# Roots as powers on GpSimd, and additional maxima spread over steps, in a four-layer fp32 kernel

## The chip, the core and the metric

The kernel runs on one core of a Trainium2 chip. The metric is the device time of one execution in microseconds. Engines are named as in the profile: PE (matrix products), DVE (vector), ACT (activation functions), POOL (GpSimd), SP (the queue that issues most transfers). PEclk is the TensorE clock that was granted, as a share of full speed.

## What is computed

Everything is fp32. The input is x of 8 batches x 512 tokens x 256 channels, and four residual layers follow one another:

```python
x = x + attn(_layernorm(x))          # ProbSparse: top 307 of 512 queries by max - mean of the scores
x = x + ffn(_layernorm(x))           # 16 blocks of 64 hidden units, the top 4 of each token
x = attn_b(x)                        # gated linear attention, then SwiGLU, each behind an RMS norm
x = x + ffn(_layernorm(x))           # the blocked FFN again
```

Square roots occur in five places: in each layernorm, `(x - m) / sqrt(v + eps)`; in the RMS norms, whose root is added to an epsilon before it divides; and in the gated linear attention, where each head's output of 16 elements is normalized:

```python
var = jnp.mean((o - mu) ** 2, axis=-1, keepdims=True)
o = (o - mu) / jnp.sqrt(var + LN_EPS)
```

In the first attention, the maximum over keys of each query's scores decides which queries are kept: the scores are computed twice, once for the maxima and once for the exponentials.

## The kernel before

**Attention** (0 to about 552 us). The work is laid out in 128 steps, one for each batch (8), half of the channels (m), every second head (e) and quarter of the queries or keys (k). A step issues four maxima, one for each of four heads (`max_one`: two matrix products at L582, then a DVE reduction at L588) for its own position, and the exponentials (`exp_one`: three products at L608, an ACT Exp at L615 into a tile of tag "e", ten buffers) of the position 16 steps earlier (LAG), and the weighing of the values (`weigh`, L630) of the position before that. Between them, piece by piece, stands `front(b)`, which prepares a later batch: the normalized x is transposed (L415), projected to queries and keys (L435), and each of these is split into a high and a low half (`halves`: ACT L446 and L452, POOL L453) in tiles of tag "half", four buffers, which transfers (SP) then move to their places. When the maxima of a group are complete, `place_maxima` turns them (POOL L548, PE L554) and writes the thresholds of the kept queries into the "top" tiles, also of tag "half" (ACT L558 and L562, POOL L570 and L571).

Which group is placed in which step is put on a list in `all_maxima`. Near the end, from step 112 on, in every fourth step four further maxima are issued in one burst behind the step's own, so that the last maxima are done some steps early. `add_bias(b)` adds the output bias to a batch's x on POOL (L398); for batches 0 to 2 it stands in step 11, for the others four steps before their front begins.

Batches 1 and later are normalized by `one_by_root`: a reciprocal root computed on POOL with an integer first guess and three Newton rounds, 14 small instructions (L278 to L286) in all. Batch 0 has a root of its own (L342), which the change leaves as it is.

**The rest** (from about 592 us). The tokens are cut in four slices k. The blocked FFN, then the gated linear attention `gla(k)`, SwiGLU and the FFN again run slice by slice; pieces of the routing of the next slices and of `gla` are put between PE's long runs of matrix products. The scheduler decides the order of the instructions on each engine at build time, and each engine works through its own in that order. PSUM buffers made by `bank_l` (two in all) serve the projections (`project`: PE L1226, ACT copy L1231, DVE gate addition L1232), the transposes of o (L1348) and others in turn.

In `gla`, `heads(m)` computes o for one half of the channels: the products and reductions of DVE, POOL and ACT, then the squares (ACT L1326), o times the gate (POOL L1327) and the sum of the squares by head (DVE L1328) into `var[:, m]`. When both halves are done, ACT takes the root of the whole of var (L1335), DVE its reciprocal (L1336), and DVE multiplies o by it (L1339), one half after the other. PE transposes o after that.

`stats` (L69, L70), which the FFNs and `gla` use, takes a root on ACT and its reciprocal on DVE; `gla` has two further roots on ACT, rr (L1171) and r2 (L1380). ACT holds the tables of one set of functions at a time; where the next function is of another set, a table load stands ahead of it.

Of the kernel before, what the change touches and what calls it, by code (L numbers as in the profile page):

```python
# [10 lines left out]
F32 = mybir.dt.float32  # L11
HALF = mybir.dt.float32r
U8 = mybir.dt.uint8
I32 = mybir.dt.int32
# [26 lines left out]
def block_kernel(ctx: ExitStack, tc: tile.TileContext, t: dict, out: bass.AP):  # L41
# [13 lines left out]
    root = keep.tile([P, 1], F32, name="root")  # L55

    nc.scalar.activation(root, eps, AF.Sqrt)
    ident = keep.tile([P, P], F32, name="ident")
    make_identity(nc, ident)

    def stats(pool, srcs, n, tag):

        st = pool.tile([P, n, 6], F32, tag=tag + "_st", name=tag + "_st")
        mv = pool.tile([P, n, 2], F32, tag=tag + "_mv", name=tag + "_mv")
        rs = pool.tile([P, n], F32, tag=tag + "_rs", name=tag + "_rs")
        for i, src in enumerate(srcs):
            nc.vector.bn_stats(st[:, i, :], src)
            nc.vector.bn_aggr(mv[:, i, :], st[:, i, :])
        nc.scalar.activation(rs, mv[:, :, 1], AF.Sqrt, bias=eps)  # L69
        nc.vector.reciprocal(rs, rs)  # L70
        return mv, rs

    def normalize(dst, src, mv, rs, i):
# [33 lines left out]
    with ExitStack() as outer:  # L107
# [75 lines left out]
        with ExitStack() as inner:  # L183
# [86 lines left out]

            def one_by_root(rs, var, scale):

                n = rs.shape[1]
                v = a1.tile([P, n], F32, tag="ln_v", name="ln_v")
                u = a1.tile([P, n], F32, tag="ln_u", name="ln_u")
                nc.gpsimd.tensor_scalar(v, var, scale, LN_EPS, ALU.mult, ALU.add)  # L278
                nc.gpsimd.tensor_scalar(
                    rs.bitcast(I32), v.bitcast(I32), -0.5, float(0x5F3759DF), ALU.mult, ALU.add  # L280
                )
                for _ in range(3):
                    nc.gpsimd.tensor_tensor(u, v, rs, ALU.mult)
                    nc.gpsimd.tensor_tensor(u, u, rs, ALU.mult)
                    nc.gpsimd.tensor_scalar(u, u, -0.5, 1.5, ALU.mult, ALU.add)
                    nc.gpsimd.tensor_tensor(rs, rs, u, ALU.mult)  # L286

            def sum_stats(b, late):

# [99 lines left out]
            def move(dst, src, eng):  # L389

                eng.dma_start(out=dst.bitcast(I32), in_=src.bitcast(I32))

            fronts = {}
            bo = a1.tile([P, D], F32, name="bo")

# [7 lines left out]
            def front(b, pick, alone):  # L403
# [35 lines left out]

                def halves(ps, bias, early):  # L440

                    hi, lo = (
                        a2.tile([P, L], F32, tag="half", name=f"half{b}", bufs=4)
                        for i in range(2)
                    )
                    nc.scalar.activation(hi.bitcast(HALF), ps, AF.Identity, bias=bias)  # L446
                    if early:
                        nc.vector.scalar_tensor_tensor(
                            lo.bitcast(HALF), ps, bias, hi, ALU.add, ALU.subtract
                        )  # L450
                    else:
                        nc.scalar.activation(lo, ps, AF.Identity, bias=bias)  # L452
                        nc.gpsimd.tensor_tensor(lo.bitcast(HALF), lo, hi, ALU.subtract)  # L453
                    return hi, lo
# [86 lines left out]
            def place_maxima(b, m, es, tiles=range(4)):  # L541


                pt = bank_m(f"mxT_ps{b}")
                ks = slice(tiles[0], tiles[-1] + 1)
                cols = slice(P * ks.start, P * ks.stop)
                for e in es:
                    nc.gpsimd.tensor_copy(  # L548
                        apart.rearrange("p k (j r) -> p k j r", r=32)[:, ks, :, 2 * e : 2 * e + 2],
                        mx[:, b % 2, m, e, :].rearrange("p (k j) -> p k j", j=4)[:, ks]  # L550
                        .unsqueeze(3).to_broadcast([P, len(tiles), 4, 2]),
                    )
                for k in tiles:
                    nc.tensor.transpose(pt[:, bass.ts(k, P)], apart[:, k, :], ident)  # L554
                whole, hi = (
                    a2.tile([P, L], F32, tag="half", name=f"top{b}", bufs=4) for i in range(2)
                )
                nc.scalar.mul(whole[:, cols], pt[:, cols], -1.0)  # L558
                for e in es:
                    r = row_of(b, m, e)  # L560
                    nc.sync.dma_start(out=neg[r : r + 4, cols], in_=whole[2 * e :: 32, cols])
                nc.scalar.mul(hi[:, cols].bitcast(HALF), pt[:, cols], -1.0)  # L562

                top = tops[(2 * b + m) % 3][:, cols].bitcast(HALF)
                if b == NB - 1:
                    nc.vector.scalar_tensor_tensor(
                        top, hi[:, cols], less_odd, whole[:, cols], ALU.mult, ALU.add
                    )
                else:
                    nc.gpsimd.tensor_scalar(hi[:, cols], hi[:, cols], less_odd, None, ALU.mult)  # L570
                    nc.gpsimd.tensor_tensor(top, hi[:, cols], whole[:, cols], ALU.add)  # L571
# [146 lines left out]
                    place_maxima(*full.pop(0)[1])  # L718

            coming = 0  # L720

            def all_maxima(step):

                nonlocal coming
                coming += 1
                b, m, e, k = step
                if coming > len(steps) - 2:
                    full.append((n + 1, (b, m, (e,), (range(3), range(3, 4))[k - 2])))
                elif k == 3 and b == NB - 1 and m == 1:
                    full.append((n + 2, (b, m, (e,))))  # L730
                elif k == 3 and e == 1:
                    full.append((n + 2, (b, m, (0, 1))))
                if coming == len(steps):
                    place_full(n + 2)
                    top_queries()

            for n in range(len(steps) + LAG + 1):
# [32 lines left out]
                if here is not None:  # L770
                    last_exps = es[3][0:1, 0:1]
                if ahead is not None:
                    all_maxima(ahead)
                    if n >= 112 and n % 4 == 0 and coming < len(steps):
                        ahead = steps[coming]
                        together([max_one(*ahead, i, bank_m) for i in range(4)])
                        all_maxima(ahead)

                if n < FIRST:
                    if n in loads:  # L780
                        load_after(loads[n], maximum_of(n))
                    if n in (2, 5):
                        clear_values(n // 2, maximum_of(n))
                    if n == 1:
                        for _ in early[1]:
                            pass
                    if n > 1:
                        next(early[2], None)
                    if n == 9:
                        nc.gpsimd.tensor_copy(bo[0:1, 0:1], maximum_of(n))  # L790
                        nc.sync.dma_start(out=bo, in_=t["L0_attn_a_bo"].partition_broadcast(P))
                    if n == 11:
                        for b in range(3):
                            add_bias(b)
                    if n == 12:
                        build_spread(maximum_of(n))
                    while done < 22 * (n + 1) // FIRST:
                        next(pieces, None)
                        done += 1
                else:  # L800
                    if n >= LAG:
                        next(later, None)
                    if i == 12 and 0 <= batch < NB - 3:
                        norm(batch + 3)
                        add_bias(batch + 3)
                    if i == 0 and 0 <= batch < NB - 2:
                        pieces = front(batch + 2, bank_m, False)
                    if not empty:
                        next(pieces, None)
# [352 lines left out]
    def heads_of(x, axis="n"):  # L1162
        return x.rearrange(f"p {axis} (h d) -> p ({axis} h) d", d=DH)

    def gla(k):
# [2 lines left out]
        yield  # L1168

        rr = small("rr")  # L1170
        nc.scalar.activation(rr, mv[:, :, 1], AF.Sqrt)  # L1171
        nc.vector.tensor_tensor(rr, rr, rs, ALU.mult)
        nc.vector.tensor_scalar(rr, rr, RMS_EPS, None, ALU.add)
        nc.vector.reciprocal(rr, rr)
# [94 lines left out]
        def heads(m):  # L1269
# [56 lines left out]
            nc.scalar.activation(sq, o[m], AF.Square)  # L1326
            nc.gpsimd.tensor_tensor(o[m], o[m], gate, ALU.mult)  # L1327
            nc.vector.tensor_reduce(var[:, m, :], heads_of(sq), AX.X, ALU.add)  # L1328
            yield


        var = rest.tile([P, NC2, NB * P // DH], F32, tag="var", name="var")
        for m in range(NC2):
            yield from heads(m)
        nc.scalar.activation(var, var, AF.Sqrt, bias=eps, scale=1.0 / DH)  # L1335
        nc.vector.reciprocal(var, var)  # L1336
        oT = rest.tile([P, 2, NC2, 512], F32, tag="made", name="oT")
        for m in range(NC2):
            nc.vector.tensor_tensor(  # L1339
# [37 lines left out]
        r2 = small("r2")  # L1377
        nc.vector.tensor_tensor(r2, mv[:, :, 0], mv[:, :, 0], ALU.mult)
        nc.vector.tensor_tensor(r2, r2, mv[:, :, 1], ALU.add)
        nc.scalar.activation(r2, r2, AF.Sqrt)  # L1380
        nc.vector.tensor_scalar(r2, r2, RMS_EPS, None, ALU.add)
        nc.vector.reciprocal(r2, r2)
        yield
# [111 lines left out]
```

## Time and profile before

| | us |
|---|---|
| three runs: median (lowest to highest) | 1603.43 (1598.21 to 1610.94) |
| the profiled execution, its time | 1599.7 |
| the profiled execution, its span | 1598.0 |
| mean granted clock of the profiled execution | 0.98 |
| a table load on ACT | 1.283 |
| reduction of var, 128x64 from 128x1024, DVE (L1328) | 1.22 |
| reciprocal of var, 128x128, DVE (L1336) | 0.95 |
| root of var, 128x128, ACT (L1335) | 0.40 |

In the lines of the profile, a group of instructions is named by its line, its engine and what it writes from what it reads. "<-" in square brackets names what ended the idle time ahead of an instruction. A line of the waits says which instruction waited for which other: microseconds in all, how many times, the longest. A line of the busy table gives for a stretch of time what each engine was busy, the number of its instructions in brackets, and then PEclk, the share of the transfer engines and GB/s.

### The profile page before, as it was taken

What the parts mean: (1) busy time and instruction counts of PE and PEld (TensorE: products, weight loads), DVE (VectorE), ACT (ScalarE), POOL (GpSimd) and SP (SyncE); (2) the same over time, 40 slices, a digit from 0 to 9 for tenths busy, and PEclk for the clock granted to TensorE, in tenths of its full rate; (3) what the DMA queues carried; (4) which work ended last, traced back from release to release, by engine and by line L of the source; (5) the groups of instructions that cost most, each with busy time, mean ns of one, the idle gap of its engine ahead of it and who ended that gap; (6) DMA issues with size and microseconds to landing.
All of it is one profiled execution on the core that took longest, in us unless ns stands there. A gap on an engine that the chain in (4) does not pass through costs nothing.

```text
span 1598.0 us, 21558 instructions
## 1 busy us (share of the span) xinstructions
PE 1547.5 (97%) x7982; PEld 860.5 (54%) x7982; DVE 943.9 (59%) x1974; ACT 704.5 (44%) x1290; POOL 454.5 (28%) x547
## 2 busy tenths in 40 slices
PE   6799999999999999999999999999999999999999
PEld 3344444444444376655564556546545655767666
DVE  6688776776776974547744566467275532354332
ACT  4377777677765843442255225432631542221110
POOL 4653453452220241123433233234243210000000
PEclk9899999999996999999999999999999999999999
DMA  5301112112110051100000001000000010011100
GB/s 188 122 16 68 42 42 81 42 42 81 42 42 2 3 171 27 40 2 13 1 0 0 0 2 27 0 0 1 1 1 1 0 28 1 23 31 40 40 27 27
DMA packets 38553, 52.65 MB, mean 33 GB/s; under 512 B 9068, under 2 KB 22580, under 8 KB 38448
## 3 DMA queue, kind: packets, MB, share of 16 engines
q1 hardware_dynamic: 37648, 50.09, 9.6%
q8 instruction: 63, 1.03, 0.3%
q10 hardware_dynamic: 800, 1.18, 0.2%
q14 instruction: 42, 0.34, 0.1%
HBM read 21.24 MB, written 4.33 MB: 16 GB/s over the span
## 4 chain that ended last, share of the span: by engine, by line
PE 78%; DVE 11%; ACT 4%; POOL 4%; issue 2%; DMA 2%; SPq 0%; ACTq 0%; POOLq 0%; DVEq 0%
PE y_ps L1087 17%; PE h_ps L1113 11%; PE s L608 10%; PE av L630 8%; PE swi_ps L1140 8%; PE proj_ps L1226 7%; PE s L582 5%; DVE pr L1259 2%; PE v_ps L505 2%; DVE pr L1249 2%; PE gla_y L1356 2%; PE q_ps L435 2%; PE k_ps L435 2%; POOL o L1276 1%; PE chT_ps L944 1%
## 5 line engine op out<-in xcount | busy, mean ns | idle before, releaser
L588 DVE TENSOR_REDUCE mx<-s 128x1 f32<-128x512 f32 x512 | 325.8, 684 | 119.2 <-PE s L582 118.1
L615 ACT ACTIVATE e<-s 128x512 f32<-128x512 f32 x512 | 276.0, 600 | 127.5 <-PE s L608 121.1
L1087 PE MATMUL y_ps<-w,h 128*128 128x256 f32 x1024 | 236.6, 387 | 8.2 <-DVE h L1122 7.6
L1113 PE MATMUL h_ps<-xnT,w 128*128 128x512 f32 x512 | 228.2, 594 | 0.0
L1087 PEld LDWEIGHTS y_ps<-w,h 128*128 128x128 f32 x1024 | 194.8, 193 | 48.8 <-DVE h L1122 13.2
L1113 PEld LDWEIGHTS h_ps<-xnT,w 128*128 128x128 f32 x512 | 94.7, 190 | 105.8 <-issue 103.8
L630 PE MATMUL av<-e,va 128*32 128x512 f32 (+1 forms) x1216 | 148.7, 559 | 2.1 <-ACT st L640 2.0
L582 PE MATMUL s<-km,qh 32*128 32x512 f32 x512 | 137.5, 508 | 8.5 <-DMA km<-half 4.4
L1121 ACT ACTIVATE h<-h_ps,b 128x512 f32<-128x512 f32 x96 | 65.3, 685 | 176.7 <-PE h_ps L1113 176.7
L1122 DVE TENSOR_TENSOR h<-h,mk 128x512 f32<-128x512 f32 x128 | 94.1, 749 | 82.7 <-ACT h L1121 62.0
L608 PE MATMUL s<-qh,km 32*128 32x512 f32 x512 | 139.4, 508 | 0.9 <-ACT e L615 0.8
L1098 DVE TENSOR_TENSOR xres<-xres,y_ps 128x512 f32<-128x512 f32 x47 | 32.2, 685 | 155.1 <-PE y_ps L1087 117.9
L1140 PE MATMUL swi_ps<-zT,w_up 128*128 128x512 f32 x256 | 122.4, 597 | 0.3 <-DVE h L1149 0.3
L1140 PE MATMUL swi_ps<-zT,w_gate 128*128 128x512 f32 x256 | 121.6, 593 | 0.0
L1087 PE MATMUL y_ps<-w_down,h 128*128 128x256 f32 x512 | 117.5, 380 | 0.0
L1226 PE MATMUL proj_ps<-q_w,rT 128*128 128x512 f32 x256 | 115.3, 594 | 0.5 <-ACT al L1209 0.4
L608 PE MATMUL s<-ql,km 32*128 32x512 f32 x512 | 112.9, 408 | 0.0
L608 PE MATMUL s<-tops,takes 4*128 4x512 f32 x512 | 110.3, 402 | 0.0
L582 PE MATMUL s<-km,ql 32*128 32x512 f32 x512 | 110.2, 412 | 0.0
L582 PEld LDWEIGHTS s<-km,qh 32*128 32x128 f32 x512 | 55.5, 187 | 101.5 <-DVE mx L588 68.4
L1087 PEld LDWEIGHTS y_ps<-w_down,h 128*128 128x128 f32 x512 | 95.1, 190 | 19.0 <-issue 7.4
L1146 ACT ACTIVATE h<-swi_ps 128x512 f32<-128x512 f32 x64 | 38.1, 595 | 139.9 <-PE swi_ps L1140 139.7
(235 smaller groups left out, 2186.9 us busy)
## 6 DMA issues: line engine op xcount, KB each, us to landing
mk<-md SPq DMA_DIRECT2D x32, 256.0 KB
qh<-half SPq DMA_DIRECT2D x63, 128.0 KB
ql<-half SPq DMA_DIRECT2D x63, 128.0 KB
km<-half SPq DMA_DIRECT2D x63, 128.0 KB
out<-xres SPq DMA_DIRECT2D x15, 256.0 KB
xres<-in_L_attn_a_x SPq DMA_DIRECT2D x7, 512.0 KB
w<-in_f_w1T SPq DMA_DIRECT2D x1, 1024.0 KB
w<-in_f_w2T SPq DMA_DIRECT2D x1, 1024.0 KB
```

The source lines that it names most:

```text
L435: nc.tensor.matmul(ps, w[:, c, bass.ts(m, P)], x[:, c, :], start=(c == 0), stop=(c == NC2 - 1),)
L582: nc.tensor.matmul(s, (qh, ql)[i].bitcast(HALF)[rows, e, bass.ts(k, P)], km.bitcast(HALF)[rows, e, :], start=(i == 0), stop=(i == 1),)
L588: nc.vector.tensor_reduce(mx[:, b % 2, m, e, r : r + 1], s, AX.X, ALU.max)
L608: nc.tensor.matmul(s, keys.bitcast(HALF), queries.bitcast(HALF), start=(i == 0), stop=(i == 2),)
L615: nc.scalar.activation(ex, s, AF.Exp, scale=1.0 / DH**0.5)
L630: nc.tensor.matmul(av[32 * j : 32 * j + 32, queries], va[:, 8 * kt + 4 * m + j, DH * e : DH * e + 2 * DH], es[j][:, queries], start=(kt == ...
L1087: nc.tensor.matmul(y[0][:, bass.ts(i, D)], h[f][:, bass.ts(2 * u + i, P)], w[:, f, :], start=(f == 0), stop=(f == NF - 1),)
L1113: nc.tensor.matmul(ps, w1[:, c, bass.ts(f, P)], xT[g][:, c, :], start=(c == 0), stop=(c == NC2 - 1),)
L1121: nc.scalar.activation(hf, ps, AF.Relu, bias=b1[:, f : f + 1])
L1122: nc.vector.tensor_tensor(hf, hf, mk[g][:, f, :], ALU.mult)
L1140: nc.tensor.matmul(ps, w[:, c, bass.ts(f, P)], zT[g][:, c, :], start=(c == 0), stop=(c == NC2 - 1),)
L1226: nc.tensor.matmul(ps, rT[b // G4][:, c, bass.ts(b % G4, P)], q_w[:, c, m], start=(c == 0), stop=(c == NC2 - 1),)
```

## The change

All roots but those of batch 0's normalization become powers on POOL: `to_power(x, p)` raises a tile to 0.5 or -0.5 in place, with the exponent as a tile that is broadcast. `one_by_root` shrinks to two instructions. The root of var is taken for each m on its own, right behind its reduction. The root activation of ACT and the reciprocal of DVE go in `stats` and for var; for rr and r2 the root goes, and the reciprocal stays.

In the attention, the halves tiles of batches 0 and 1 and the first pair of top tiles use the buffers of tag "e". The further maxima are issued one a step (two from step 120 on) instead of four in every fourth, with the placement of the last batch's first half one step later. The biases of batches 0 to 2 are added in steps 18, 22 and 26 instead of 11.

```diff
+    def to_power(x, p):
+
+        nc.gpsimd.tensor_tensor(x, x, p.to_broadcast(list(x.shape)), ALU.pow)
+
...
-        nc.scalar.activation(rs, mv[:, :, 1], AF.Sqrt, bias=eps)
-        nc.vector.reciprocal(rs, rs)
+        nc.gpsimd.tensor_scalar(rs, mv[:, :, 1], LN_EPS, None, ALU.add)
+        to_power(rs, less_half)
...
-                n = rs.shape[1]
-                v = a1.tile([P, n], F32, tag="ln_v", name="ln_v")
-                u = a1.tile([P, n], F32, tag="ln_u", name="ln_u")
-                nc.gpsimd.tensor_scalar(v, var, scale, LN_EPS, ALU.mult, ALU.add)
-                nc.gpsimd.tensor_scalar(
-                    rs.bitcast(I32), v.bitcast(I32), -0.5, float(0x5F3759DF), ALU.mult, ALU.add
-                )
-                for _ in range(3):
-                    nc.gpsimd.tensor_tensor(u, v, rs, ALU.mult)
-                    nc.gpsimd.tensor_tensor(u, u, rs, ALU.mult)
-                    nc.gpsimd.tensor_scalar(u, u, -0.5, 1.5, ALU.mult, ALU.add)
-                    nc.gpsimd.tensor_tensor(rs, rs, u, ALU.mult)
+                nc.gpsimd.tensor_scalar(rs, var, scale, LN_EPS, ALU.mult, ALU.add)
+                to_power(rs, less_half)
...
+            def half_tile(first, name):
+
+                tag, bufs = ("e", 10) if first else ("half", 4)
+                return a2.tile([P, L], F32, tag=tag, name=name, bufs=bufs)
...
-                    hi, lo = (
-                        a2.tile([P, L], F32, tag="half", name=f"half{b}", bufs=4)
-                        for i in range(2)
-                    )
+                    hi, lo = (half_tile(alone, f"half{b}") for i in range(2))
...
-                whole, hi = (
-                    a2.tile([P, L], F32, tag="half", name=f"top{b}", bufs=4) for i in range(2)
-                )
+                whole, hi = (half_tile(b + m == 0, f"top{b}") for i in range(2))
...
-                    full.append((n + 2, (b, m, (0, 1))))
+                    full.append((n + 2 + b // (NB - 1), (b, m, (0, 1))))
...
-                    all_maxima(ahead)
-                    if n >= 112 and n % 4 == 0 and coming < len(steps):
-                        ahead = steps[coming]
-                        together([max_one(*ahead, i, bank_m) for i in range(4)])
+                    if n >= 112 and n % 4 == 0 and coming + 1 < len(steps):
+                        extra = [(*steps[coming + 1], i) for i in range(4)]
                         all_maxima(ahead)
+                        all_maxima(steps[coming])
+                    else:
+                        all_maxima(ahead)
+
+                    for _ in range(2 if n >= 120 else 1):
+                        if extra:
+                            together([max_one(*extra.pop(0), bank_m)])
...
-                    if n == 11:
-                        for b in range(3):
-                            add_bias(b)
...
+                    if n in (18, 22, 26):
+                        add_bias((n - 18) // 4)
...
-        nc.scalar.activation(rr, mv[:, :, 1], AF.Sqrt)
+        nc.gpsimd.tensor_copy(rr, mv[:, :, 1])
+        to_power(rr, half_power)
...
             nc.vector.tensor_reduce(var[:, m, :], heads_of(sq), AX.X, ALU.add)
+            nc.gpsimd.tensor_scalar(
+                var[:, m, :], var[:, m, :], 1.0 / DH, LN_EPS, ALU.mult, ALU.add
+            )
+            to_power(var[:, m, :], less_half)
             yield
...
-        nc.scalar.activation(var, var, AF.Sqrt, bias=eps, scale=1.0 / DH)
-        nc.vector.reciprocal(var, var)
...
-        nc.scalar.activation(r2, r2, AF.Sqrt)
+        to_power(r2, half_power)
```

In the changed build, SP's order of transfers is the same as before; table loads on ACT number 20 instead of 45.

## The prediction

> **What bounds the kernel now.** I read the page first (shares, slices), then the busy table by stretch, then the waits of PE, then the timelines of DVE, POOL and ACT around each root.
>
> ```profile
> span 1598.0 us, 21558 instructions
> PE 1547.5 (97%) x7982; PEld 860.5 (54%) x7982; DVE 943.9 (59%) x1974; ACT 704.5 (44%) x1290; POOL 454.5 (28%) x547
> PE   6799999999999999999999999999999999999999
> PEclk9899999999996999999999999999999999999999
> ```
>
> PE is the bound: 97% busy, so only some 50 us of it stand idle, and beside them there is the time in which it is busy at a lower clock (slices 1 and 12). ACT, from which the change takes work, is 44% busy. A gain can come only from PE's idle time and from its clock. The stretches that hold both (columns: PE, PEld, DVE, ACT, POOL busy, granted clock):
>
> ```profile
> 50.00:55.00 5.00, 3.93 (x18) 1.34 (x16) 3.86 (x9) 1.19 (x2) 3.93 (x17) 1.00 0.76 260
> 55.00:60.00 5.00, 0.73 (x8) 0.28 (x6) 3.52 (x6) 1.19 (x3) 3.70 (x4) 0.92 0.60 165
> 60.00:65.00 5.00, 4.87 (x16) 3.03 (x17) 0.00 (x0) 1.89 (x5) 4.78 (x6) 0.50 0.42 158
> 480.00:482.00 2.00, 1.34 (x10) 0.48 (x9) 1.40 (x3) 0.42 (x1) 0.00 (x0) 1.00 0.01 4
> 486.00:511.00 25.00, 24.69 (x154) 10.19 (x150) 13.16 (x23) 12.60 (x25) 1.17 (x3) 0.50 0.01 2
> ```
>
> The waits of PE (us in all, times, longest), and from ACT's timeline the wait behind one of them:
>
> ```profile
> PE xnT_ps L415 <- DVE xn L319: 6.7, 1, 6.7
> PE v_ps L505 <- ACT half L452: 4.4, 1, 4.4
> PE oT_ps L1348 <- DVE o L1339: 4.4, 2, 2.5
> PE s L582 <- DVE mx L588: 2.5, 4, 0.8
> PE xnT_ps L415 <- POOL xn L319: 2.0, 4, 1.3
> 58.81 0.69 ACT L446 ACTIVATE half<-q_ps,bq 128x512 fp32r<-128x512 f32 x1 [5.77 <-POOL tops L571]
> ```
>
> The 6.7 us wait is the first load and stays. The other 13.3 us are what the change can reach.
>
> **The change part by part** (against the profiled execution: 1599.7 us, span 1598.0; the median of the three runs is 1603.4, 3.7 more, which I add at the end).
>
> *Table loads.* The order of the changed kernel has 20 loads in place of 45: 25 x 1.283 us (the row of L1335's loads) = 32 us of ACT. ACT is nowhere the engine that PE waits for in these stages (its waits above are on DVE and POOL), so I cost this at 0. The cover is ACT's 56% of free time. The Trainium skill ("ScalarE: Activation LUTs", What ACT_TABLE_LOAD costs) puts a switch at 2.66 us, load and drain; the timeline has the load at 799.44 and the root at 800.73, 1.29 later, with no drain to see. By the page 66 us of ACT would go, by the trace 32; at 0 on the path both give 0.
>
> *Start, one_by_root.* Fourteen POOL instructions (0.20 each, 0.28 apart, 3.8 us from 49.64 to 53.60; for batch 1 with a halves product between them, 29.95 to 35.01) become two. At 35.0 xn of batch 1 comes about 2 us earlier, which takes most of PE's 2.0 us wait on POOL xn. *Halves.* At 53.10 ACT is ready for batch 1's halves, but all four "half" buffers are held until POOL's tops L571 ends at 58.78: ACT waits 5.77, PE 4.41 (55.7 to 60.13), and the clock is then 0.50 until about 66 and near 0.57 from 72 to 80. In tag "e" (ten buffers, no exponential yet alive) this wait goes. Next late is DVE: four maxima take 2.48 us a step and DVE is otherwise full from 36 to 56, so a floor remains; the maxima of step 16, which end at 75.4 now, I put at 65. The biases (2.37 us each on POOL, three in a row from 61.95) hold up batch 1's second halves product (68.90) and its values (70.12), for which PE's weighing waits in turn. In the changed order of POOL the product stands ahead of them, the values between them (two biases, two value additions, the third bias, two more), so that cover is only partly gone: 2 x 2.37 still lie ahead of the first value. SP's order is unchanged; no transfer is moved past another. Start in all: -10, with -6 (DVE binds at once) and -13 (the second low-clock stretch goes too) as ends.
>
> *Additional maxima.* Now four come in one burst at n=112, 116, 120, so DVE has eight in a row (8 x 0.62 = 5.0 us in a 3.2 us step), and PE waits 2.5 us in all. One a step is 5 x 0.62 = 3.1, under the step; two at n=120 and 121 are 3.7, over it by 0.5 each. So -2.5 + 1 from waits. After the third burst the clock goes to 0.50 from 482.5 to 511, where a step takes 5.1 us, not 3.2: some five steps, 9.5 us. The skill ("TensorE: Matmul & The Clock Gate", What's actually happening) lowers the clock after an idle window of about 3.4 us and gives it back after as much busy time. The row has 0.56 us idle ahead of the fall, and then 29 us at half clock with PE busy 24.69 of 25.00, so here the rule is not what decides. By the rule I would leave the stretch in and book -1.5; by the trace, where the only thing ahead of the fall is the burst, -11. I take -11 and keep -1.5 as an end.
>
> *var, the part that costs.* From the timelines of DVE and POOL at the first heads group of the second slice:
>
> ```profile
> 894.06 1.22 DVE L1328 TENSOR_REDUCE var<-sq 128x64 f32<-128x1024 f32 x1 [1.43 <-ACT sq L1326]
> 895.20 0.68 DVE L1149 TENSOR_TENSOR h<-h,swi_ps 128x512 f32<-128x512 f32 x1
> 895.79 0.52 DVE L1232 TENSOR_TENSOR gate<-proj_ps,bog 128x128 f32<-128x128 f32 x2
> 894.11 2.36 POOL L1327 TENSOR_TENSOR o<-o,gate 128x1024 f32<-128x1024 f32 x1 [1.17 <-ACT sq L1326]
> ```
>
> In the changed order DVE's multiplication of o[0] by var (1.22 us) comes directly behind this reduction, ahead of the h product and of the gate additions, which free PE's projection banks. It needs POOL: o*gate ends at 896.47, then scale-and-eps on 128x64 (0.2), then the power on 128x64, X. So DVE stands still from 895.3 to 896.75+X, multiplies until 897.97+X, does h (0.6) and a gate addition (0.29): PE, which takes the bank at 897.02 now, gets it at 898.9+X, 1.9+X later. The same sum at the other three slices gives 0.9+X (the first, squares from 743.58), 1.8+X (the third, PE at 1055.58) and 1.9+X (the fourth, PE at 1195.93): 6.5+4X. PE is in order, so this is idle time with no cover.
> For the second half (m=1) the old way is root (0.40, its load hidden), reciprocal 0.95 and two multiplications of 1.18; the new way is POOL's o*gate, scale, X, one multiplication. It is done at S+5.05+X, where S is the start of the squares (797.79, 966.19, 1102.70, 1243.68). But PE's transposes of o stand earlier in the changed order. At 1102.70 PE is there at 1104.2 and would wait 3.6+X, against 1.9 now; at 966.19 it is there at 969.2 and waits 2+X, against nothing. All four: 0.5, 2, 1.7, 0 = 4.2+4X. After such gaps the clock can fall: it stayed 1.00 after the 1.9 us at 1106 and was 0.57 for 4 us after the 2.5 us at 1247.5. I add 3.
>
> *X, a power on 128x64.* No row shows a power. Below: plain POOL rows of this size, between L286 on 128x16 (224 ns) and L356 on 128x128 (400 ns), 0.3 us. Above: the skill ("GPSIMD Engine Reference", Performance pitfalls) has a dependent fp32 chain at 4 cycles a step, and a power is a logarithm and an exponential; with twenty such steps for each of 64 columns and nothing overlapped, at the page's 1.2 GHz, that is 4.3 us (an estimate; the twenty are my assumption). The ends are far apart; I take the value by the nearest row and double it, 0.6, because more is computed than an addition.
>
> *Other roots.* stats, rr and r2 swap an ACT root and DVE reciprocal (0.30 + 0.20 us) for two small POOL instructions (0.2 + a power on 8 columns, which at 0.2 to 0.8 us is under the 0.5 + load removed). They may queue behind POOL's L995 additions (1.29 us). Bounds -2 to +4 over twelve groups; I take 0.
>
> Sum: -10 - 11 + 6.5 + 4.2 + 3 + 8 x 0.6 = -2.5. 1599.7 - 2.5 + 3.7 = 1601.
>
> **The rivals.**
> *The stalls in the recurrent layer don't come (0.32).* If PE has a free bank when I say it waits, or arrives later at the transposes because it was delayed before, only the gains of the attention part are left: -21 and at most a third of the 18.5: 1603.4 - 15 to - 21, about 1585. For it: in these stages PE now waits for 4.4 us in all on o, and DVE is only 57% busy from 640 to 1280, so gaps were absorbed before. Against it: the orders of DVE and PE are fixed, and PE has no other work to take ahead.
> *The power is slow (0.28), the side of slower.* One mechanism: X sits eight times on PE's path in the recurrent layer. The time is 1603.4 - 7.3 + 8X; it passes the time before at X = 0.9 us and the 1% bound at X = 2.9. At X = 3, 1620; at 4.3, 1630. POOL's own load speaks neither way: it is 28% busy. [...] If a power ran element by element behind branches, the loss would have no such bound; I leave that to the remainder.
> *The low clock stays after 482 or moves (inside the forecast and the rival above).* Then +9.5: 1610.
>
> **How the numbers follow.** Forecast case 0.40: gains and losses cancel, 1592 to 1613, likeliest 1601. A difference of 1% (16 us: under 1587.4, over 1619.5) is about what a measurement of this kernel can tell from none. The first rival lies mostly under 1587.4, the slow power about half to two thirds over 1619.5, and a slow power together with a low clock that stays is over it from X = 1.7. So faster 0.32, same 0.40, slower 0.28. The range runs from 1579 (all gains, no stall) to 1628 (X = 4), which leaves out some 2 in 10, nearly all above.
>
> **What would show it.** The L65 power rows on POOL: at 128x64, 0.3 to 1 us agrees, over 3 means the slow case. PE's waits: "v_ps <- ACT half" gone, "oT_ps <- DVE o" grown from 4.4 to about 13, new waits of proj_ps behind DVE gate additions near 897, 1056 and 1196 of about 2.5 us each. Clock 1.00 in 60 to 68 and in 486 to 511 shows the gains. If the stretch from 640 to 1280 is not longer by about 18 us, my reading of the changed order was wrong; if the first 80 us are not shorter by 6 at least, DVE's maxima were the bound there all along.

## The result, and the profile after

The changed kernel takes 1725.44 us (1721.4 to 1732.46) where the kernel before takes 1605.2: a ratio of 1.0754, 95% interval 1.0701 to 1.0807, some 120 us slower. The forecast was 1601, and the range ended at 1628. The rival with the slow power is what happened, at a price of the power beyond the bound that was set for it.

From the page of the changed kernel (busy times, and the slices of PE and its clock):

```profile
span 1719.7 us, 21462 instructions
...
PE 1559.9 (91%) x7982; PEld 867.6 (50%) x7982; DVE 937.3 (55%) x1958; ACT 667.4 (39%) x1241; POOL 570.3 (33%) x553
...
PE   6999999999999899968797979786987699999999
...
PEclk8999999999999999979898989988998899999999
```

PE does the same work, is idle for 160 us instead of 50, and is busy for 12 us longer, at a lower clock. The idle slices and the dips of the clock stand together in the middle of the row, in the stretch with the recurrent layer. ACT lost 37 us and POOL gained 116; neither is near full. The waits of PE (us in all, times, longest) say who holds it:

```profile
PE proj_ps L1229 <- DVE gate L1235: 54.8, 5, 15.5
PE oT_ps L1353 <- DVE o L1344: 50.3, 4, 14.2
PE y_ps L1089 <- DVE h L1124: 7.6, 5, 2.8
PE s L579 <- DMA ql<-half: 6.6, 1, 6.6
PE xnT_ps L417 <- DVE xn L316: 6.4, 1, 6.4
PE chT_ps L946 <- ACT row L934: 6.1, 4, 1.6
PE chT_ps L946 <- DVE xnT L950: 5.2, 2, 2.9
```

The first line is new, and the second was 4.4 us. Both name DVE, but DVE's own rows are as short as before. What DVE waits for is the power, in its list of waits:

```profile
DVE o L1344 <- POOL var L65: 93.8, 8, 12.2
```

In POOL's groups by shape (count, busy us, mean ns):

```profile
L65 POOL TENSOR_TENSOR var<-var,less_half 128x64 f32<-128x64 f32 x8 | 84.2, 10529 | 0.7
...
L65 POOL TENSOR_TENSOR ln_rs<-ln_rs,less_half 128x8 f32<-128x8 f32 x12 | 19.9, 1659 | 0.5
...
L65 POOL TENSOR_TENSOR r<-r,half_power 128x8 f32<-128x8 f32 x4 | 6.6, 1646 | 2.0 <-DVE r L1384 2.0
L65 POOL TENSOR_TENSOR rr<-rr,half_power 128x8 f32<-128x8 f32 x4 | 6.5, 1632 | 0.0
...
L65 POOL TENSOR_TENSOR ln_rs<-ln_rs,less_half 128x4 f32<-128x4 f32 x3 | 3.1, 1044 | 0.2
L65 POOL TENSOR_TENSOR ln_rs<-ln_rs,less_half 128x16 f32<-128x16 f32 x1 | 2.9, 2925 | 0.1
```

X is 10.53 us, not 0.6. The four sizes of less_half (4, 8, 16 and 64 columns) lie on a line, about 0.16 us for each column and 0.4 for the instruction; the addition of the kernel before on 128x128 (L356) took 0.40 in all. The place that the prediction worked through, the first half of the second slice, in the three timelines (start, duration, and in brackets the idle time before and what ended it). POOL:

```profile
915.44 2.35 POOL L1330 TENSOR_TENSOR o<-o,gate 128x1024 f32<-128x1024 f32 x1 [1.17 <-ACT sq L1329]
917.88 0.24 POOL L1332 TENSOR_SCALAR var<-var 128x64 f32<-128x64 f32 x1
918.21 10.53 POOL L65 TENSOR_TENSOR var<-var,less_half 128x64 f32<-128x64 f32 x1
```

DVE:

```profile
915.39 1.22 DVE L1331 TENSOR_REDUCE var<-sq 128x64 f32<-128x1024 f32 x1 [1.43 <-ACT sq L1329]
928.78 1.23 DVE L1344 TENSOR_TENSOR o<-o,var 128x1024 f32<-128x1024 f32 x1 [12.16 <-POOL var L65]
929.92 0.68 DVE L1151 TENSOR_TENSOR h<-h,swi_ps 128x512 f32<-128x512 f32 x1
930.51 0.48 DVE L1235 TENSOR_TENSOR gate<-proj_ps,bog 128x128 f32<-128x128 f32 x2
```

PE:

```profile
917.03 1.88 PE L1142 MATMUL swi_ps<-zT,w_gate 128*128 128x512 f32 x4
930.86 6.48 PE L1229 MATMUL proj_ps<-q_w,rT 128*128 128x512 f32 x8 [11.95 <-DVE gate L1235]
```

POOL computes the power while DVE stands for 12.16 us in front of the multiplication that needs it. The gate additions queued behind that multiplication were ready: ACT's copies out of the same banks, which come before them, ended at 917.71. PE waits 11.95 us for the bank that they free (the prediction's 1.9 + X with the measured X gives 12.4). Then eight matmul records take 6.48 us where as many take 3.60 at full clock (granted clock 0.50 from 925 to 935).

### The profile page after: what moved, and what is told of

It reads as the page before. It is cut to its first block, busy times and chain, and to the rows that moved or that the text cites. A ratio compares the mean times of both kernels' runs of the same rounds, so it can differ in the third digit from the quotient of the medians.

```text
span 1719.7 us, 21462 instructions
## 1 busy us (share of the span) xinstructions
PE 1559.9 (91%) x7982; PEld 867.6 (50%) x7982; DVE 937.3 (55%) x1958; ACT 667.4 (39%) x1241; POOL 570.3 (33%) x553
## 4 chain that ended last, share of the span: by engine, by line
PE 66%; DVE 13%; POOL 13%; ACT 4%; issue 2%; DMA 1%; SPq 1%; POOLq 0%; DVEq 0%; ACTq 0%
PE y_ps L1089 13%; PE h_ps L1115 9%; PE s L605 9%; PE av L627 8%; PE proj_ps L1229 6%; PE swi_ps L1142 5%; POOL var L65 5%; PE s L579 4%; DVE pr L1262 3%; DVE pr L1252 3%; POOL o L1279 3%; DVE w L1254 2%; PE q_ps L437 2%; PE v_ps L504 2%; PE k_ps L437 2%
## 5 line engine op out<-in xcount | busy, mean ns | idle before, releaser
L1089 PE MATMUL y_ps<-w,h 128*128 128x256 f32 x1024 | 232.3, 382 | 8.2 <-DVE h L1124 7.6
L1229 PE MATMUL proj_ps<-q_w,rT 128*128 128x512 f32 x256 | 127.8, 644 | 55.3 <-DVE gate L1235 54.8
L627 PE MATMUL av<-e,va 128*32 128x512 f32 (+1 forms) x1216 | 145.1, 546 | 2.0 <-ACT st L637 2.0
L1229 PEld LDWEIGHTS proj_ps<-q_w,rT 128*128 128x128 f32 x256 | 52.0, 206 | 120.7 <-DVE gate L1235 63.1
```

The costliest lines, as they stand in the source:

```text
L627: nc.tensor.matmul(av[32 * j : 32 * j + 32, queries], va[:, 8 * kt + 4 * m + j, DH * e : DH * e + 2 * DH], es[j][:, queries], start=(kt == ...
L1089: nc.tensor.matmul(y[0][:, bass.ts(i, D)], h[f][:, bass.ts(2 * u + i, P)], w[:, f, :], start=(f == 0), stop=(f == NF - 1),)
L1229: nc.tensor.matmul(ps, rT[b // G4][:, c, bass.ts(b % G4, P)], q_w[:, c, m], start=(c == 0), stop=(c == NC2 - 1),)
```

## The experiments

Ratios are against the kernel before, in the runs of the same chip; microseconds worked out from them use 1603. PE does the same 7982 products in every run, so what differs between two profiles is its idle time (waits) and its busy time (mostly the clock). The mean granted clock of each execution is also on record; one minus that clock, times the span, serves below as an estimate of the time lost to a low clock. It counts idle time at a low clock too, so it is an upper estimate.

**The attention parts alone.** Every root back as before:

```diff
-        nc.gpsimd.tensor_scalar(rs, mv[:, :, 1], LN_EPS, None, ALU.add)
-        to_power(rs, less_half)
+        nc.scalar.activation(rs, mv[:, :, 1], AF.Sqrt, bias=eps)
+        nc.vector.reciprocal(rs, rs)
...
-            to_power(var[:, m, :], less_half)
...
+        nc.scalar.activation(var, var, AF.Sqrt, bias=eps, scale=1.0 / DH)
+        nc.vector.reciprocal(var, var)
```

(and the same for one_by_root, rr and r2)

> The attention parts alone, every root as before. Theory (the power of var costs 10.5 us on PE's path eight times, and the attention parts gain what the changed profile shows, 17 us up to the out projection): 1586 to 1590, a ratio of about 0.99. Rival (half of those 17 us come from the two-instruction roots of batches 1 and 2, not from the buffers and the maxima): 1594 to 1597. Rival (the gains are given back later in the order): 1603.

1592.4 us, ratio 0.9921 (0.9885 to 0.9957): -13 us, between the theory and its first rival. The third, that the gains are given back, falls.

**The attention parts with the short one_by_root.** As above, but one_by_root keeps its two instructions.

> The attention parts and the short one_by_root (powers on 4 and 16 columns), the roots of the four slices on ACT as before. Theory: the powers on 4 columns take 1.04 us where 14 instructions took 3.8, and xn of batches 1 and 2 is in PE's path at the start: 1583 to 1588, at or a few us below the run without them. Rival (short roots are hidden behind the loads): the same within 2 us.

1585.47 us, ratio 0.9877 (0.9839 to 0.9915), -20 us: faster than both kernels. On 4 columns a power of 1.04 us and one instruction of 0.20 take the place of 14 in 3.8 us. The intervals of this run and the one before overlap. The executions of the two, on one chip, hardly do (1583.3 to 1589.5 against 1588.6 to 1596.3): their means differ by 6 us, with 2 and 11 as ends.

**var back on ACT, the small powers left.** In the changed kernel only var's root and reciprocal are put back.

> The changed kernel with only var's root and reciprocal back on ACT and DVE; stats, rr, r2 and one_by_root stay powers. Theory (var's wait on PE's path: 105 us of PE waits less the 4 of before, and about 3 us of half clock after each of eight gaps): 1600 to 1608. Rival (POOL is loaded too much by powers in general; var's are 84 of 123 us of them): about 1630. What is left over the run with all slice roots on ACT is the price of the small powers: theory 10 to 18 us, mostly where PE waits on the rows ahead of the channel transposes.

1632.62 us, ratio 1.0149 (1.0095 to 1.0202). The wait for var goes: 1.0754 to 1.0149 is 97 us, give or take 12. But what is left is 44 us above the run without powers in the slices, more than twice what the theory allowed; the time is the rival's 1630. The rival's cause, a POOL that is too full, fits less well: POOL is busy for 30% of this run. Against the profile of the run without powers in the slices, PE is idle for 29 us more and busy for 17 us longer. Its waits of this run that are new or grown (the gate had 0.4 us there, the channel transposes none):

```profile
PE proj_ps L1229 <- DVE gate L1235: 10.0, 2, 7.6
PE chT_ps L946 <- DVE xnT L950: 6.8, 3, 2.9
PE chT_ps L946 <- ACT row L934: 6.4, 4, 1.6
PE mT_ps L1057 <- DVE taken L1050: 3.3, 3, 1.4
PE swi_ps L1142 <- DVE h L1151: 3.1, 3, 1.4
```

How one comes about shows in DVE's timeline of this run at the first slice:

```profile
747.69 0.17 DVE L928 SCALAR_TENSOR_TENSOR ln_sh<-ln_mv,ln_rs 128x8 f32<-128x8 f32 x1 [2.34 <-POOL ln_rs L65]
749.30 0.17 DVE L1175 TENSOR_TENSOR rr<-rr,ln_rs 128x8 f32<-128x8 f32 x1 [1.44 <-POOL rr L65]
750.89 0.17 DVE L928 SCALAR_TENSOR_TENSOR ln_sh<-ln_mv,ln_rs 128x8 f32<-128x8 f32 x1 [1.43 <-POOL ln_rs L65]
...
755.36 0.28 DVE L1235 TENSOR_TENSOR gate<-proj_ps,bog 128x128 f32<-128x128 f32 x1
```

and PE's:

```profile
746.25 1.88 PE L1229 MATMUL proj_ps<-q_w,rT 128*128 128x512 f32 x4
755.69 2.08 PE L1229 MATMUL proj_ps<-q_w,rT 128*128 128x512 f32 x2 [7.57 <-DVE gate L1235]
```

In the kernel before, at the same place, DVE waits 0.37 us for a root, and PE goes on without a wait:

```profile
741.36 0.20 DVE L70 RECIPROCAL ln_rs<-ln_rs 128x8 f32<-128x8 f32 x1 [0.37 <-ACT ln_rs L69]
743.57 3.60 PE L1226 MATMUL proj_ps<-q_w,rT 128*128 128x512 f32 x8
```

Three powers stand one behind the other on POOL (746.00, 747.63, 749.23), DVE waits for each in turn, and the gate addition that PE needs comes after all three: small waits of 1.4 to 2.3 us on DVE become one of 7.57 on PE. Part of the way leads over ACT: its copy out of the same bank (754.09) stands behind the squares (753.13), and these wait for a DVE instruction that comes after the powers.

**All powers, none of the attention parts.** The kernel before with the five kinds of power put in.

> The kernel before with all the powers and none of the attention parts. Theory: the parts are additive, 1735 to 1745. Rival (attention parts gain nothing of their own): 1725.

1733.77 us, ratio 1.0797 (1.0747 to 1.0847). The medians leave 8 us between this and the changed kernel, where the attention parts alone gave 13; the intervals of the ratios (this one and 1.0701 to 1.0807) overlap, so this run does not decide whether the parts are additive.

**var with a cheap instruction.** The power of var becomes a multiplication, in the same place; the kernel leaves the root out:

```diff
-            to_power(var[:, m, :], less_half)
+            nc.gpsimd.tensor_tensor(
+                var[:, m, :], var[:, m, :], less_half.to_broadcast([P, NB * P // DH]), ALU.mult
+            )
```

> The changed kernel with a POOL multiplication by -0.5 in place of the power of var, in the same place and order; the root of var is left out, so the layer's heads are not normalized. X falls from 10.5 to about 0.3 us, everything else (the early multiplication of o on DVE, the small powers) stays. Theory (X on PE's path eight times, with half clock behind the long gaps): 1620 to 1645. If the order alone costs what the prediction put for it (10.7 us at X = 0), it lies about 12 above the 1632.6 of the run with var back on ACT; if the order costs nothing, at 1632 or below. Rival (the loss sits in the order, not in X): 1690 and more.

1637.64 us, ratio 1.0220 (1.0163 to 1.0277). With X at 0.29 us all but 11 us of var's cost is gone (0.0071 above the run with var on ACT, with nothing and some 24 us as ends). PE's waits say the same; in the run with var on ACT these two were 10.0 and 4.4:

```profile
PE proj_ps L1229 <- DVE gate L1235: 16.6, 4, 7.6
PE oT_ps L1355 <- DVE o L1346: 9.5, 4, 3.9
```

So the new order by itself costs some 11 us; the prediction's 10.7 + 8 x 0.3 = 13 fits.

**A third of the columns.** The other 42 columns get no root.

```diff
-            to_power(var[:, m, :], less_half)
+            to_power(var[:, m, 0:22], less_half)
```

> The changed kernel with the power on 22 of the 64 columns of var; the other 42 keep their variance, so their heads are not normalized. Theory (0.16 us a column and 0.2, so X = 3.8, and 8 to 8.6 us of time for each us of X from the 1637.6 at X = 0.3): 1660 to 1668. Rival (a power instruction has a fixed price whatever its columns): about 1725. If the half clock comes only behind gaps of over some 4 us, the lower end.

1670.64 us, ratio 1.0416 (1.0380 to 1.0453). Its power, in POOL's groups:

```profile
L65 POOL TENSOR_TENSOR var<-var,less_half 128x22 f32<-128x22 f32 x8 | 30.8, 3848 | 0.7
```

The time lies some 3 us over the theory's range. So three points for the same order: X of 0.29, 3.85 and 10.53 us, ratios 1.0220, 1.0416 and 1.0754. From the first to the second that is 31 us for 3.56 (8.8 us of time a us), from the second to the third 54 for 6.68 (8.1). Over all it is 8.4, with 7.1 and 9.6 as ends, which the prediction's 8X fits. A fixed price of the instruction falls.

**The first half later.** One DVE instruction ties the first half's multiplication to the second half's var:

```diff
         for m in range(NC2):
             yield from heads(m)
+        nc.vector.scalar_tensor_tensor(
+            var[:, 0, 0:1], var[:, 1, 0:1], 0.0, var[:, 0, 0:1], ALU.mult, ALU.add
+        )
```

> The changed kernel with one more DVE instruction of one column, which adds nothing to var but ties the first half's multiplication of o to the second half's var: DVE no longer stops behind the first half's power. POOL does the same work. Theory (DVE standing still ahead of the gate additions is what holds PE): the 54.8 us of PE's waits on the gate go, with some 12 us of half clock behind them, and the second half's wait grows by about 1.5 us each for one multiplication more: 1655 to 1670. Rival (POOL is the engine that is missing for 10.5 us): 1715 to 1725.

1680.66 us, ratio 1.0499 (1.0416 to 1.0582): 41 us come back, give or take 16, while POOL does every power that it did. The time is 11 us above the theory's range; with this interval, it is not shown that anything is missing. The waits of PE:

```profile
PE oT_ps L1356 <- DVE o L1347: 50.4, 4, 15.0
PE proj_ps L1229 <- DVE gate L1235: 9.6, 2, 7.6
```

45.2 of the 54.8 us on the gate are gone. The 9.6 left are the two of the small powers (the run with var back on ACT has 10.0). So for the first half it was not POOL's time that was missing: what cost was an instruction waiting at the head of DVE's queue. For the second half's 50 us PE does wait for the power itself, through the multiplication behind it.

**rr and r2 only.** The changed kernel with var and stats back on ACT:

> The changed kernel with var and stats back on ACT and DVE: of the slices' powers only rr and r2 on 8 columns are left (eight of 1.65 us). The run with the twelve powers of stats as well took 1632.6, the run with none 1585.5. Theory (stats are the start of each slice's routing and recurrent chain, and DVE waits for their powers 18.5 us): stats carry two thirds, so 1597 to 1605. Rival (r2, between the layer and SwiGLU, carries them): 1615 to 1625.

1599.17 us, ratio 0.9986 (0.9950 to 1.0023). Between this and the run without slice powers (0.9877) lie 17 us for rr and r2, give or take 8; between it and the run with stats as powers (1.0149) lie 26 us for stats, give or take 10. The theory's two thirds lie within that.

**stats with a cheap instruction.** In the run with var back, stats multiplies where it took the power; the kernel leaves these roots out:

```diff
-        to_power(rs, less_half)
+        nc.gpsimd.tensor_tensor(rs, rs, less_half.to_broadcast(list(rs.shape)), ALU.mult)
```

> The changed kernel with var back on ACT, and in stats a POOL multiplication by -0.5 in place of the power: the roots of stats are left out, the route over POOL and the order of every engine are those of the run with var back (1632.6). The power's 1.66 us becomes about 0.2. Theory (DVE stands behind the power in front of the shift, 1.7 us in 10 of 12 groups, and the work behind it on DVE holds PE): 1600 to 1612. Rival (the detour over POOL, its queue and the new order cost as much as the power itself): 1618 to 1628.

1603.67 us, ratio 0.9999 (0.9971 to 1.0027). So 24 of the 26 us, give or take 10, are the length of the power (1.66 us against 0.20, twelve times: 17.5 us on POOL), and the detour over POOL shows no cost. PE's wait on the gate falls from 10.0 to 3.5 us in this run.

**The halves in the ten buffers, alone.**

> The kernel before with the halves of batches 0 and 1 and the first tops in the ten buffers, nothing else. Theory (the wait of ACT on four buffers and the 4.4 us of PE behind it at 56 us, with half clock after): 1595 to 1599, most of the 13 us of all the attention parts. Rival (DVE's maxima bound the start anyway): 1602 to 1606.

1600.05 us, ratio 0.9969 (0.9932 to 1.0007). By the times, the gain of 5 us can't be told from none. The profile shows what went: PE's 4.4 us wait of the values' product on ACT's halves is not in it, PE is idle for 3.1 us less, and busy as long as before. The time less the estimate for the low clock is 5 us shorter over the ten executions, give or take 2.

**The further maxima one a step, alone.**

> The kernel before with the further maxima one a step, nothing else. Theory (a half-clock stretch of 10 to 29 us follows short waits by chance, and stood at other places in the profiles of the runs so far, so the burst is not its cause; only the burst's own 2.5 us of waits go): 1598 to 1602 beside 1602, a gain of 1 to 4. Rival (the burst brings the half clock at 482 us, as the prediction had it): 1589 to 1593.

1596.39 us, ratio 0.9941 (0.9911 to 0.9971): 9.5 us, with 4.7 and 14 as ends. That is over the theory's 1 to 4 and within the rival's 9 to 13. The waits on the maxima in the last steps fall from 1.6 to 0.3 us, but one of 1.1 us for turning the maxima is new there; over the whole profile PE is idle for 1.8 us less. It is busy for 6.3 us less with the same products (1541.2 against 1547.5), so most of the gain is clock. The executions agree: the mean granted clock is 0.982 in the 11 of this run and 0.977 in 27 of the kernel before, by the estimate 8.5 us less lost to a low clock, give or take 5. In this the rival is right. Its place and its cause are not shown. Time lost to low clock from 430 to 560 us (summed over slices of 5 us, one minus the granted clock) was 15.3 us in the profile of the kernel before, but 3.4 in each of the three other kernels that still have the bursts, and 1.7 to 5.1 in the ten without. So the bursts do not bring the long stretch each time; where and why the clock is higher on the mean stays open.

**The biases later, alone.**

```diff
-                    if n == 11:
-                        for b in range(3):
-                            add_bias(b)
...
+                    if n in (18, 22, 26):
+                        add_bias((n - 18) // 4)
```

> The kernel before with the biases of batches 0 to 2 in steps 18, 22 and 26, nothing else. All attention parts together gave a ratio of 0.992, the halves alone 0.997. Theory (three biases in a row on POOL, 7 us, stand ahead of batch 1's second halves product and its values): a gain of 1 to 5, 1597 to 1601. Rival (ACT's wait for the buffers comes first and hides it): within 1 us of the kernel before.

1609.53 us, ratio 1.0036 (1.0004 to 1.0068): a little slower, which neither side expected. On POOL one bias still stands ahead of the first value and all three ahead of the last two, which end at 74.34 us (72.91 before), so no gain was due. The loss goes with the clock: on the mean of the 12 executions it is 0.973 against 0.977, by the estimate 7 us, give or take 6. Why it is lower is not known.

## Why the prediction was wrong

**The step that failed: the size of X.** "I take the value by the nearest row and double it, 0.6" was 10.53. The nearest row was of another operation. The two rows it was read from rise by 1.6 ns for each further column (0.224 us at 16, 0.400 at 128), the power by 158; a multiplication put in the power's place took 0.29 us. No row of the trace before had any bearing on it. The upper end, twenty dependent steps at the 4 cycles of the Trainium skill ("GPSIMD Engine Reference", Performance pitfalls for Q7 kernels), gave 4.3, and the twenty were a guess: by an estimate with the clock of 1.2 GHz that the same page gives (Specifications), the measured price is some 190 cycles a column. The range took its upper edge, X = 4, from that guess, so it was too low with it. The prediction did name a power without such a bound, and left it to what lies outside its range. With X = 10.53 its own formula, 1603.4 - 7.3 + 8X, gives 1680; the other 45 us to the measured 1725 are about what the small powers cost.

**The second: the small powers at 0.** They were put at "0.2 to 0.8 us" on 8 columns and measured 1.65; their cost was 44 us (17 for rr and r2, 26 for stats, rounded), where the prediction's upper bound was 4. It also took a reciprocal off rr and r2, where only the root goes. With the measured lengths the step's own terms, so corrected, give 28 us: 12 x (0.2 + 1.66 - 0.5) for stats, 4 x (0.2 + 1.63 - 0.3) for rr, 4 x (1.65 - 0.3) for r2. That is close to the 29 us of more idle time on PE; beside them PE was busy for 17 us longer at a lower clock, a term the step did not have. And it did not look for the way by which short waits of DVE reach PE, three in a row in front of one gate addition: it had applied this to var and not to the roots beside it.

**Right: the places and the slope.** PE's waits that var brought were foreseen as 6.5 + 4X and 4.2 + 4X beside the 4.4 of before, 48.6 and 50.7 us at the measured X. The profile has 54.8 less the 9.6 to 10.0 of the small powers, so about 45, and 50.3. The slope of 8 was measured as 8.4, with 7.1 and 9.6 as ends. At the measured X its terms for var sum to 13.7 + 84, 98 us, where 97 were measured. Tying the first half to the second removed the first of the two waits and left the second.

**Right in sum, in part by luck: the attention.** -21 was booked for the attention parts and the short one_by_root, and -20 was measured for them. But 9.5 of the -11 for the maxima was the half-clock stretch of a single execution, at a place where three other kernels with the same bursts do not have it. That the maxima gave 9.5 all the same, through the clock but at no place that the profiles show, is luck as far as is known. The halves, the biases and the short roots were to give -10 together: the halves' wait went as described, and the three measure about -5, +6 and -7, each give or take some 5.

**Right, as far as it was measured: the table loads at 0.** ACT became 37 us less busy. No run takes loads away and nothing else. The nearest is stats with a cheap instruction: against the run with stats on ACT it has 25 loads instead of 39 and ACT is busy for 21 us less, and its ratio is 0.9999 against 0.9986, so the fewer loads bought nothing that shows. (PE's waits on ACT from 592 us on were not nil, as the prediction had it, but 1.4 us.)

In steps from one kernel to the next, by ratio: attention and short roots -20, rr and r2 +17, stats +26, var +97. That these make the +120 is so by construction; each step was measured with the others as they stood.

## What to carry to other kernels

An operation that no row of the trace shows has no nearest row: measure it by itself, at two sizes, before anything is built on it, or let the range run as far as the worst case would. For an engine that works through its queue in order, the question of a new wait is not whether the awaited engine has time, but which instruction behind the waiting one somebody else needs; ask it of the small instructions too. A stretch of low clock in one profile is not yet the cost of what stands ahead of it; before a few us are explained by waits, compare the mean granted clock of all executions.

## What the runs showed of the hardware

A power on POOL took 1.04, 1.66, 2.93, 3.85 and 10.53 us on 4, 8, 16, 22 and 64 columns of 128 partitions. It gained some 6 us where it replaces fourteen instructions on 4 columns (and one such chain on 16), and lost in the slices: 44 us on 8 columns, 97 on 64.

The clock fell to half behind a wait of 0.4 us, in the midst of work. The busy table of the run with the attention parts and the short roots (length, then PE, PEld, DVE, ACT, POOL busy, granted clock):

```profile
380.00:385.00 5.00, 5.00 (x43) 2.08 (x42) 2.88 (x5) 3.15 (x6) 4.56 (x4) 1.00 0.33 121
385.00:390.00 5.00, 4.58 (x34) 1.83 (x38) 2.97 (x6) 3.81 (x7) 1.28 (x1) 0.95 0.32 121
390.00:395.00 5.00, 5.00 (x40) 1.96 (x36) 2.29 (x5) 1.77 (x4) 0.21 (x1) 0.50 0.14 52
395.00:400.00 5.00, 5.00 (x34) 1.74 (x36) 2.17 (x4) 2.66 (x5) 0.77 (x1) 0.52 0.01 2
400.00:405.00 5.00, 5.00 (x49) 2.57 (x41) 3.88 (x7) 3.40 (x8) 0.00 (x0) 1.00 0.02 3
```

PE had been busy without a gap at clock 1.00 since 120 us, waited 0.4 us once (for ACT's halves, at 388 us), and ran at half clock from 390 to 400. By the rule that the prediction weighed, an idle window of about 3.4 us ("TensorE: Matmul & The Clock Gate" of the Trainium skill, What's actually happening), the clock would have stayed up; by the trace these 10 us lost 5. At this place the same happened in all five profiles in which that wait was 0.4 to 0.8 us, and in none of the nine in which it was 0.2 us or absent. But it is no rule: in the kernel before, waits of 0.5 and 0.6 us between 440 and 470 us left the clock at 1.00, and the next of 0.56 was followed by 29 us of half clock. Between 430 and 560 us such stretches cost a single profile from 1.7 to 15 us, a spread as large as what the attention parts are worth together.
